# Two graph layers on one core: the first graph's index lists beside the last graph of layer 0, fewer small VectorE operations, and another plan for layer 1

## The chip, the cores and the metric

One core of a Trainium2 chip runs the whole program. The metric is the device time of one execution in microseconds (us), as a median of several runs. Beside it stands one profiled execution, from which every duration of a single instruction comes. The engines are TensorE (PE; its weight load is listed apart as PEld), VectorE (DVE), ScalarE (ACT), GpSimd (POOL) and SyncE (SP, which here only starts transfers). Each engine works through its own instructions in a fixed order and stands still where one of them waits.

## The reference

Two layers are applied in turn to 16 graphs of 1024 nodes with 256 features, each as `x = layernorm(x + layer(x, adj))`. The adjacency is a 0/1 matrix for each graph, about 0.4% ones, denser among the low node numbers.

```python
def layer0(h, adj):                       # h: 16 x 1024 x 256
    Wh = h @ W.T
    att = bn(Wh @ a1 [:, :, None] + Wh @ a2 [:, None, :])
    att = bn(where(att >= 0, att, 0.2 * att))
    att = softmax(att, axis=2) * adj
    return elu(bn(att @ Wh))

def layer1(inputs, adj):                  # 4 heads
    coefs_adj = softmax(adj, axis=-1)
    def head(Wh, w1h, b1h, w2h, b2h, ah, bh):
        fts = inputs @ Wh
        logits = (fts @ w1h + b1h)[:, :, None] + (fts @ w2h + b2h)[:, None, :]
        coefs = ah * softmax(leaky_relu(logits, 0.2) - 1e9 * (1 - adj)) + (1 - ah) * coefs_adj
        return elu(coefs @ fts + bh + inputs)
    return mean over the heads
```

`bn` of the last line of layer 0 takes its mean and variance over all graphs and nodes, so layer 1 of the first graph can only be worked on when the last graph of layer 0 is through.

## The kernel before

**Sizes.** `P` = 128 nodes make a block, `K` = 8 blocks a graph, `C` = 2 halves of the 256 features, `H` = 4 heads, `KH` = 4 blocks half a graph. The adjacency stands in DRAM in bf16 (`adj16`).

**Layer 0** (up to line 662) works in dense form. For each graph 16 steps `n` run (two halves of the nodes, eight blocks each): `aggregate` (line 585, PE, products into `pa`) for this graph, `weights` (538 to 556, ACT and DVE) for the next. A dense transposed mask is loaded two graphs ahead. Tile, the scheduler, orders the instructions here by the program's order and their dependences. After the last `store` (593) lines 648 to 662 make the scale `s3` and shift `t3` of the batch norm.

**Layer 1** is sparse. For every block of 128 target nodes the source nodes that have any edge into it are listed, and padded to whole chunks of 128: `CAPS` = (6, 4, 3, 3, 3, 3, 2, 2) chunks for the eight blocks, 26 in a graph. The lists are made on the chip, for each graph in two halves: `load_rows` (SP) brings rows of `adj16`, `counts` (PE, `pc`) and `used` (DVE) tell which source has an edge into which block, `places` (PE, `pp`) and `placed` (DVE) give each its place, eight `mark` (DVE, line 1153) spread the places as one-hot tiles, `pick` (PE, `pl`) turns these into node numbers, and `indices` (DVE) writes them to `ix` and `im`. With these, POOL's indirect DMAs fetch for each chunk 128 rows of the table `xe_dram` (`fetch_rows`, line 1194, tile `xc`) and 128 mask rows (`fetch_mask`, line 1202, tile `mc`); both have 20 buffers. The masks are rows of `mt_dram`, an f32 copy of the transposed adjacency that POOL's `store_mask` writes from the tile `mt`, of which there is one buffer, filled by a transposing load of SP (`load_mask`).

The table holds, for each node, `x` after layer 0 (lines 1231 to 1346 prepare it: `exps`, `elu`, `turn` with PE's `pz` at line 1250, `residual` with DVE lines 1260 to 1265, `means`, `squares`, `spans` with POOL's power at line 1285, `norm`, `factors`, `raised`, `scale`, `table`, `total`), a one, and exponentials of the attention terms. `rows` brings the targets' factors (`A`, SP), `larger` (ACT, line 1221) and `weights` (DVE, line 1225, tile `w`, 12 buffers) make the edge weights of a chunk for four heads. `neighbours` (PE, line 1347, `pm`) sums each target's neighbours, with the number of them in column 257; `summed` (DVE, 1354 and 1355) and `shares` (DVE, 1359 to 1372) make from it the share of `softmax(adj)`.

**Units.** Each block takes two units of two heads each, 16 (`NU`) for a graph and 256 in all. A unit passes through `gather` (PE, line 1414, `pu`, two PSUM buffers), `share` (ACT, 1424), `sums`, `invert`, `mix` (DVE, 1431 to 1441), `turn` (PE, 1450, `pt`, one buffer), `turned` (ACT, 1456), `linear` (PE, 1462, `pv`, one buffer), `add` (DVE, 1469), `exps` (ACT, 1473), `sum` (DVE, 1480 to 1488), `squares` (ACT), `span` (DVE), `power` (POOL, 1516 and 1517), `close` (ACT, 1523) and `store` (SP, 1529). `addends` (POOL, line 1401, tile `v`) makes x plus bias ahead of `add`.

**The order of layer 1 is written out by hand** (`manual_schedule`): every engine runs its instructions in program order. One turn of the loop near the end is one unit number `n`; it takes the steps of units `n` to `n - 9` in a fixed order, and at three places (`stand(0)`, `stand(1)`, `stand(2)`) the side steps that prepare later graphs, from the lists `early`, `first` and `after`. The side steps of a graph have unit numbers from -30 (30 units before its first) to 15. `turned(n, f, then)` puts PE's step `f` into `first[n]` and its reader on DVE or ACT, `then`, into `early[n + 1]`. All PSUM results of side steps (`pc`, `pp`, `pl`, `pz`, `pm`, `pA`, `pX`) share two buffers (`ps_s`), so such a step waits for the reader of the last but one before it. The weights of a chunk stand in `early`:

```python
after[-7 + 2 * it + j] += [each(g.fetch_mask, c), each(g.fetch_rows, c)]
after[-3 + 2 * it + j] += [each(g.larger, c)]
early[-2 + 2 * it + j] += [each(g.weights, c)]
```

(`it` is the block, `j` the half of its chunks.) Graphs are taken in reverse by `stand`: a later graph's steps stand ahead of an earlier one's.

Of the kernel before, what the change touches and what calls it, by code (L numbers as in the profile page):

```python
# [19 lines left out]
P = 128  # L20
# [7 lines left out]
def kernel(  # L28
# [182 lines left out]


    with ExitStack() as l0:
# [316 lines left out]
        with tc.tile_pool(name="wk", bufs=1) as wk, tc.tile_pool(  # L530
            name="ps_a", bufs=4, space=PSUM
        ) as ps_a, tc.tile_pool(name="ps_s", bufs=2, space=PSUM) as ps_s:
# [85 lines left out]
            if B > 1:  # L618
                queries(1)
            ready1 = {}  # L620
            for b in range(B):
                for n in range(NH * K):
# [6 lines left out]
                    if n == 1:  # L629
                        if b + 2 < B:  # L630
                            mts[b + 2] = mask(mpool, b + 2, "mt0")
                        elif b + 1 == B:
                            ready1[0] = mask(m1pool, 0, "mt1")
                    if n == 1 and b > 0:
                        store(b - 1, NH - 1)
# [402 lines left out]
    with ExitStack() as l1:  # L1038
# [20 lines left out]
        class Graph:  # L1059


            def __init__(self, b):
                self.b = b
                self.S, self.mr, self.xc, self.mc, self.A, self.w = ({} for _ in range(6))
                self.pz, self.pm = {}, {}

# [8 lines left out]

            def load_rows(self, hf):

                self.rw = pk.tile([P, KH, N], BF16, tag="rw", name=f"rw_{self.b}_{hf}", bufs=2)
                nc.sync.dma_start(
                    self.rw, adj16[self.b].rearrange("(q p) j -> p q j", p=P)[:, hf * KH : (hf + 1) * KH]  # L1080
                )
# [12 lines left out]


            def counts(self, hf):

                self.pc = ps_s.tile([P, K, KH], F32, tag="s", name=f"pc_{self.b}_{hf}")
                for k in range(K):
                    for q in range(KH):  # L1100
                        nc.tensor.matmul(
                            self.pc[:, k, q : q + 1], self.rw[:, q, k * P : (k + 1) * P],
                            ones16[:, 0:1], start=True, stop=True,
                        )

            def used(self, hf):

                if hf == 0:
                    self.act = pk.tile([P, K, K], BF16, tag="act", name=f"act_{self.b}", bufs=2)
                nc.vector.tensor_scalar(  # L1110
                    self.act[:, :, hf * KH : (hf + 1) * KH], self.pc, 1.0, None, ALU.min
                )

            def places(self):

                self.pp = pp = ps_s.tile([P, K + 1, K], F32, tag="s", name=f"pp_{self.b}")
                for k in range(K + 1):
                    for kk in range(min(k, K)):
# [563 lines left out]
```

## Time and profile before

| what | value |
|---|---|
| three runs, us | 2762.07, 2766.53, 2776.94 |
| median, us | 2766.53 |
| the profiled execution's own time, us | 2762.28 |
| its span (first to last instruction), us | 2760.0 |
| granted TensorE clock, mean | 0.936 |
| PE, busy us and share of the span | 2452.3, 89% |
| PEld | 1944.1, 70% |
| DVE | 2363.1, 86% |
| ACT | 1832.2, 66% |
| POOL | 1371.1, 50% |
| HBM traffic, GB/s over the span | 172 |

The costliest groups of instructions, with their line, engine, number, busy time and the mean of one:

| line, engine, what | count | busy us | mean ns |
|---|---|---|---|
| 1414 PE, `gather` into `pu` | 3328 | 798.8 | 393 |
| 1225 DVE, `weights` | 1664 | 538.0 | 392 |
| 1221 ACT, `larger` | 1664 | 510.8 | 387 |
| 1462 PE, `linear` into `pv` | 2048 | 489.3 | 382 |
| 585 PE, layer 0's `aggregate` | 1024 | 450.9 | 598 |
| 1202 POOL, `fetch_mask` | 416 | 441.9 | 1062 |
| 1194 POOL, `fetch_rows` | 416 | 418.3 | 1006 |
| 1401 POOL, `addends` | 256 | 305.0 | 1191 |

How to read the profile: a line of a timeline gives the start and the length in us, the engine, the line of the code, the operation, the tile written and those read, the shape, and `xN` where N like instructions in a row are put together; in brackets stands how long the engine was idle before it, and for whom. `L1414` is line 1414. In the list of waits, "PE pz L1250 <- DVE deg L1355: 73.7, 13, 7.0" reads: PE's work on `pz` at line 1250 waited for DVE's `deg` of line 1355, 73.7 us in all, 13 times, at most 7.0. Busy shares are means over stages that have different limits, so each stage is read for itself. The clock in such rows (PEclk) is what was granted to TensorE, as a share of full speed.

### The profile page before, as it was taken

How to read it: one execution, taken by the hardware profiler on the slowest of the kernel's cores; microseconds unless marked ns; L12 is line 12 of the kernel's file. 1: busy time of each engine (PE TensorE's matmuls, PEld its weight loads, DVE VectorE, ACT ScalarE, POOL GpSimd, SP SyncE). 2: the span in 40 equal slices, each digit the busy share in tenths (PEclk: the TensorE clock that was granted, in tenths of full speed). 3: DMA queues.
4: the chain of work that ended last, by engine and by line, in shares of the span. 5: the costliest groups of instructions: out<-in, count | busy, mean ns of one | idle time of the engine just before them, and what ended most of it. 6: DMA issues, size and time to landing. Idle time of an engine off the chain costs nothing. (4 is left out here: it accounts for less than half of the span.)

```text
span 2760.0 us, 44589 instructions
## 1 busy us (share of the span) xinstructions
PE 2452.3 (89%) x14119; PEld 1944.1 (70%) x14119; DVE 2363.1 (86%) x6522; ACT 1832.2 (66%) x4196; POOL 1371.1 (50%) x1442
## 2 busy tenths in 40 slices
PE   7964699999975999889998999999889998999997
PEld 6753354444443888778787887878778887877886
DVE  4347999999943899999999999899999999999997
ACT  1216677777734667677676876767677676776775
POOL 1001000000005768686775867668686775867682
PEclk9985799999976999999999999999999999999999
DMA  9979599756559656658576685756657565674331
GB/s 268 275 173 287 125 233 238 175 159 175 138 184 223 205 115 205 169 146 230 112 209 120 192 198 128 220 112 204 162 150 216 131 205 121 192 193 116 87 85 28
DMA packets 514451, 476.51 MB, mean 173 GB/s; under 512 B 284920, under 2 KB 434464, under 8 KB 508064
## 3 DMA queue, kind: packets, MB, share of 16 engines
q1 hardware_dynamic: 446272, 286.63, 40.2%
q0 software_dynamic: 66720, 184.44, 26.0%
q8 instruction: 115, 1.88, 0.3%
q10 hardware_dynamic: 1216, 2.51, 0.2%
q14 instruction: 128, 1.05, 0.1%
HBM read 304.72 MB, written 168.77 MB: 172 GB/s over the span
## 5 line engine op out<-in xcount | busy, mean ns | idle before, releaser
L1414 PE MATMUL pu<-xc,w 128*128 128x257 f32 x3328 | 798.8, 393 | 0.0
L1414 PEld LDWEIGHTS pu<-xc,w 128*128 128x128 f32 x3328 | 638.5, 198 | 85.4
L1225 DVE SCALAR_TENSOR_TENSOR w<-w,xc,mc 128x128 f32<-128x128 f32 x1664 | 538.0, 392 | 0.3 <-DMA mc<-mt_dram,im 0.3
L1462 PE MATMUL pv<-W1s,sT 128*128 128x256 f32 x2048 | 489.3, 382 | 34.1 <-DVE v L1469 31.6
L1221 ACT ACTIVATE w<-A,xc 128x128 f32<-128x128 f32 x1664 | 510.8, 387 | 12.9 <-DMA xc<-xe_dram,ix 12.9
L1194 POOL DMA_INDIRECT xc<-xe_dram,ix x416 | 418.3, 1006 | 149.0 <-issue 79.5
L1202 POOL DMA_INDIRECT mc<-mt_dram,im x416 | 441.9, 1062 | 99.3 <-issue 92.3
L585 PE MATMUL pa<-em,wh 128*128 128x512 f32 x1024 | 450.9, 598 | 17.7 <-issue 13.4
L1462 PEld LDWEIGHTS pv<-W1s,sT 128*128 128x128 f32 x2048 | 387.3, 191 | 101.0 <-DVE v L1469 46.0
L585 PEld LDWEIGHTS pa<-em,wh 128*128 128x128 f32 x1024 | 193.6, 192 | 250.2 <-issue 236.7
L1456 ACT COPY sT<-pt 128x512 f32<-128x512 f32 x256 | 148.1, 578 | 295.2 <-PE pt L1450 294.1
L1401 POOL TENSOR_TENSOR v<-x,bias 128x512 f32<-128x512 f32 x256 | 305.0, 1191 | 72.6 <-DVE z L1431 67.9
L1424 ACT ACTIVATE s<-S,q 128x256 f32<-128x256 f32 x512 | 230.1, 497 | 131.6 <-DVE q L1372 131.6
L1469 DVE TENSOR_TENSOR v<-pv,v 128x512 f32<-128x512 f32 x256 | 175.1, 684 | 77.4 <-PE pv L1462 74.5
L1441 DVE SCALAR_TENSOR_TENSOR s<-pu,z,s 128x256 f32<-128x256 f32 x512 | 224.3, 480 | 9.1 <-ACT w L1221 0.4
L1347 PE MATMUL pm<-xc,mc 128*128 128x257 f32 x832 | 209.3, 389 | 17.5 <-DMA xc<-xe_dram,ix 17.5
L1473 ACT ACTIVATE m<-v,neg 128x512 f32<-128x512 f32 x256 | 185.0, 723 | 44.0 <-DVE omv L1495 22.4
L541 ACT ACTIVATE e<-eb,c,s 128x1024 f32<-128x1024 f32 x128 | 155.0, 1236 | 79.0 <-DVE sm L555 42.7
L1347 PEld LDWEIGHTS pm<-xc,mc 128*128 128x128 f32 x832 | 155.6, 192 | 42.8 <-issue 11.5
L545 ACT ACTIVATE e<-e,v,u 128x1024 f32<-128x1024 f32 x128 | 152.3, 1229 | 22.7 <-DVE e L544 16.6
L1250 PE MATMUL pz<-IW,h 128*128 128x136 f32 x512 | 88.1, 317 | 87.5 <-DVE deg L1355 78.4
L1450 PE MATMUL pt<-ident,s 128*128 128x128 f32 x1024 | 162.0, 283 | 0.0
(260 smaller groups left out, 3593.8 us busy)
## 6 DMA issues: line engine op xcount, KB each, us to landing
mt_dram<-mt POOLq DMA_DIRECT2D x16, 4096.0 KB
x<-in_x_dram SPq DMA_DIRECT2D x32, 1024.0 KB
adj<-in_adj_dram POOLq DMA_DIRECT2D x16, 2048.0 KB
rw<-adj SPq DMA_DIRECT2D x32, 1024.0 KB
A<-a_dram SPq DMA_DIRECT2D x128, 256.0 KB
xe_dram<-x SPq DMA_DIRECT2D x16, 1060.0 KB
wh_dram<-wx SPq DMA_DIRECT2D x16, 1024.0 KB
wh<-wh_dram SPq DMA_DIRECT2D x16, 1024.0 KB
```

Of the source, the lines that this page charges most:

```text
L585: nc.tensor.matmul(acc[b, hf, oc], wh[b][:, k, oc * P : (oc + 1) * P], ems[b, k][:, hf * HALF : (hf + 1) * HALF], start=(k == 0), stop=(k ...
L1194: nc.gpsimd.indirect_dma_start(out=self.xc[c], out_offset=None, in_=xe_dram[self.b % 2], in_offset=bass.IndirectOffsetOnAxis(ap=self.ix[:, ...
L1202: nc.gpsimd.indirect_dma_start(out=self.mc[c], out_offset=None, in_=mt_dram[self.b % 3].rearrange("n (q i) -> (n q) i", i=P), in_offset=ba ...
L1221: nc.scalar.mul(w[:, h, :], self.A[it][:, h, :], self.xc[c][:, F1 + h : F1 + h + 1])
L1225: nc.vector.scalar_tensor_tensor(self.w[c][:, h, :], self.w[c][:, h, :], self.xc[c][:, F1 + H + h : F1 + H + h + 1], self.mc[c], ALU.max, ...
L1347: nc.tensor.matmul(pm, self.mc[c], self.xc[c][:, 0:F1], start=(c == cs[0]), stop=(c == cs[-1]))
L1401: nc.gpsimd.tensor_tensor(self.v2, self.g.x[:, self.it, 0:F].unsqueeze(1).to_broadcast([P, HP, F]), bias1[:, h : h + HP, :], ALU.add,)
L1414: nc.tensor.matmul(self.pu[:, hh, 0:F1], g.w[c][:, h, :], g.xc[c][:, 0:F1], start=(c == cs[0]), stop=(c == cs[-1]),)
L1424: nc.scalar.mul(self.s[:, hh], g.S[it], g.q[:, it, h0 + hh : h0 + hh + 1])
L1441: nc.vector.scalar_tensor_tensor(s[:, hh], self.pu[:, hh, 0:F], self.z[:, hh : hh + 1], s[:, hh], ALU.mult, ALU.add,)
L1462: nc.tensor.matmul(self.pv[:, hh, :], self.sT[:, hh, fc, :], W1s[:, fc, self.hp * HP + hh, :], start=(fc == 0), stop=(fc == C - 1),)
L1473: nc.scalar.activation(self.m, self.v2, AF.Exp, bias=neg1, scale=1.0)
```

## The change

1. **The lists of graph 0 in layer 0.** The steps of the lists move, unchanged, into a class `Lists` that takes its pools and the number `n` of blocks in a part. Graphs 1 to 15 use it as before (two parts of four). Graph 0's run in layer 0, in four parts of two, at steps 1 to 10 of the last graph; its row tiles take the buffers `e` of layer 0's `weights`, its PSUM tiles come from a new pool `ps_l`. The mask of graph 0 is loaded one graph earlier, and its store to `mt_dram` stands in layer 0; the mask of graph 1 is loaded at step 4 of the last graph.

2. **Mask fetches of graph 0.** The first 14 stand at unit -30, ahead of layer 1's other steps.

3. **Small operations.** The copy of `fs` out of `pz` goes from DVE to ACT (`beside`). `summed` takes all 257 columns at once: the degree stays in `S`, now made in pairs with four buffers, and `X` has the constant `N` as column 257. So the copy to `deg` and the first operation of `shares` are gone.

4. **The plan.** Unit numbers come from a table `AT`. The weights stand in a new list `late`, taken by `stand(3)`, which follows `stand(0)` and `stand(1)`; their unit numbers are the same. Others move by up to three units: `count` 0 from -25 to -23, `pick` 0 from -13 to -11, `elu` 3 and its `exps` from -23 to -22, `turn` 6 from -15 to -16, `nb` (neighbours) 3 and 4 one later, 6 one earlier, `rows` 0 and 3 to 6 one to three earlier and `rows` 1 one later, the fetches of blocks 2 to 5 one or two units away from their old ones, some `larger` by one, and `load_mask`, `load_h`, the second `load_rows`, `mark` 1 and `table` by one.

5. **The order within a unit** is another:

| before | after |
|---|---|
| turn, turned, gather, sums, add, invert, mean, span, mix, exps, stand(0), share, linear, stand(1), sum, squares, stand(2), addends, power, close, store | sums, add, invert, exps, turn, turned, gather, linear, store, mean, span, mix, stand(0), addends, stand(1), stand(3), share, sum, squares, stand(2), close, power |

The diff, cut to its core:

```diff
+    def store_mask(b, mt):
+        nc.gpsimd.dma_start(mt_dram[b % 3][0:N, :].rearrange("(k p) i -> p k i", p=P), mt)
+    class Lists:
+        def __init__(self, b, n, pool, psum, keep, rows):
+            self.b, self.n, self.pool, self.psum, self.keep, self.rows = b, n, pool, psum, keep, rows
+            self.rw, self.oh = {}, {}
+        def load_rows(self, hf):
+            self.rw[hf] = self.rows([P, self.n, N], BF16, f"rw_{self.b}_{hf}")
...
+        def pick(self, hf):
+            qs = range(hf * self.n, (hf + 1) * self.n)
...
@@ layer 0
+            lists0 = Lists(
+                0, 2, lk, ps_l, m1pool, lambda shape, dt, nm: wk.tile(shape, dt, tag="e", name=nm, bufs=4)
+            )
+            beside = {n: [] for n in range(NH * K)}
+            for part in range(K // 2):
+                beside[1] += [lambda part=part: lists0.load_rows(part)]
+                beside[1] += [lambda part=part: lists0.counts(part), lambda part=part: lists0.used(part)]
+            beside[2] += [lists0.places, lists0.placed, lambda: store_mask(0, ready1[0])]
+            for part in range(K // 2):
+                for q in (2 * part, 2 * part + 1):
+                    beside[3 + 2 * part] += [lambda q=q: lists0.mark(q)]
+                beside[4 + 2 * part] += [
+                    lambda part=part: lists0.pick(part), lambda part=part: lists0.indices(part)
+                ]
...
-                        elif b + 1 == B:
+                        elif b + 2 == B:
                             ready1[0] = mask(m1pool, 0, "mt1")
+                    if b == B - 1 and n == 4 and B > 1:
+                        ready1[1] = mask(m1pool, 1, "mt1")
+                    for step in beside[n] if b == B - 1 else ():
+                        step()
@@ residual
-                nc.vector.tensor_copy(self.fs[:, k], self.pz[k][:, :, P:TW])
+            def beside(self, k):
+                nc.scalar.copy(self.fs[:, k], self.pz[k][:, :, P:TW])
@@ totalled
-                self.X = pk.tile([P, F], F32, tag="X", name=f"X_{b}", bufs=2)
-                nc.scalar.copy(self.X, self.px)
-                self.deg = pk.tile([P, K], F32, tag="deg", name=f"deg_{b}", bufs=2)
+                self.X = pk.tile([P, F1], F32, tag="X", name=f"X_{b}", bufs=2)
+                nc.vector.memset(self.X[:, F:F1], float(N))
+                nc.scalar.copy(self.X[:, 0:F], self.px)
@@ summed
-                self.S[it] = pk.tile([P, F], F32, tag="S", name=f"S_{b}_{it}", bufs=6)
-                nc.vector.scalar_tensor_tensor(self.S[it], pm[:, 0:F], E1, self.X, ALU.mult, ALU.add)
-                nc.vector.tensor_copy(self.deg[:, it : it + 1], pm[:, F:F1])
+                if it % 2 == 0:
+                    self.S[it // 2] = pk.tile([P, 2, F1], F32, tag="S", name=f"S_{self.b}_{it}", bufs=4)
+                nc.vector.scalar_tensor_tensor(
+                    self.S[it // 2][:, it % 2], self.pm[it], E1, self.X, ALU.mult, ALU.add
+                )
@@ shares
-                nc.vector.tensor_scalar(r[:, 0], self.deg[:, part], E1, float(N), ALU.mult, ALU.add)
-                nc.vector.reciprocal(r[:, 0], r[:, 0])
-                nc.vector.tensor_scalar(r[:, 1], self.deg[:, part], 0.0, None, ALU.is_equal)
+                d = self.S[pair][:, :, F]
+                nc.vector.reciprocal(r[:, 0], d)
+                nc.vector.tensor_scalar(r[:, 1], d, float(N), None, ALU.is_equal)
@@ side
                 for j, part in enumerate(halves(it)):
                     for c in part:
-                        after[-7 + 2 * it + j] += [each(g.fetch_mask, c), each(g.fetch_rows, c)]
-                        after[-3 + 2 * it + j] += [each(g.larger, c)]
-                        early[-2 + 2 * it + j] += [each(g.weights, c)]
+                        after[AT["fetch", it, j] if g.b or c >= 14 else -EARLY] += [each(g.fetch_mask, c)]
+                        after[AT["fetch", it, j]] += [each(g.fetch_rows, c)]
+                        after[AT["larger", it, j]] += [each(g.larger, c)]
+                        late[AT["weigh", it, j]] += [each(g.weights, c)]
```

## The prediction

> **What bounds the kernel now.** I read the page's 40 slices first: layer 0 fills the first twelve (to 797 us), then a thin slice, then 27 dense ones, layer 1. All numbers are from the one profiled execution (span 2760.0, its own time 2762.28). Next came the table by stretches, over the part of layer 1 in which every graph does the same. Line 1285 runs once per graph; two of its rows, in the timeline of POOL, mark the stretch:
>
> ```profile
> 1035.78 1.68 POOL L1285 TENSOR_TENSOR rs<-rs,mhalf 128x8 f32<-128x8 f32 x1 [16.09 <-DVE r L1361]
> ...
> 2574.71 1.68 POOL L1285 TENSOR_TENSOR rs<-rs,mhalf 128x8 f32<-128x8 f32 x1 [16.43 <-DVE r L1361]
> ```
>
> These are graphs 2 and 15, so 13 periods of 118.4 us. The stretch between them:
>
> ```profile
> core 0: us, PE busy (x) PEld busy (x) DVE busy (x) ACT busy (x) POOL busy (x), PEclk, DMA share, GB/s
> 1036.00:2575.00 1539.00, 1426.62 (x8855) 1249.57 (x8854) 1429.07 (x4502) 1120.34 (x2978) 1089.68 (x1119) 0.96 0.65 168
> ```
>
> Divided by 13, PE is busy 109.7 and DVE 109.9 of 118.4; ACT 86.2, POOL 83.8. Two engines share the bound, and each idles 8.5 us per graph. The list of waits of the same stretch says for whom (total, times, longest):
>
> ```profile
> PE pz L1250 <- DVE deg L1355: 73.7, 13, 7.0
> DVE v L1469 <- PE pv L1462: 65.1, 69, 1.4
> ...
> PE pv L1462 <- DVE v L1469: 24.1, 22, 1.7
> ```
>
> Per graph PE waits 5.7 us once, and DVE waits 5.0 us in five pieces. The timelines of PE and DVE at the end of graph 2's units show the single wait:
>
> ```profile
> 1228.21 0.63 PE L1250 MATMUL pz<-IW,h 128*128 128x136 f32 x4
> 1235.84 1.25 PE L1250 MATMUL pz<-IW,h 128*128 128x136 f32 x4 [7.00 <-DVE deg L1355]
> 1236.88 1.06 PE L1450 MATMUL pt<-ident,s 128*128 128x128 f32 x4
> 1237.73 6.33 PE L1414 MATMUL pu<-xc,w 128*128 128x257 f32 x24
> ```
>
> ```profile
> 1229.02 0.16 DVE L1269 TENSOR_SCALAR mv<-mv 128x4 f32<-128x4 f32 x1
> 1229.09 6.21 DVE L1225 SCALAR_TENSOR_TENSOR w<-w,xc,mc 128x128 f32<-128x128 f32 x12
> 1235.21 0.41 DVE L1354 SCALAR_TENSOR_TENSOR S<-pm,X 128x256 f32<-128x256 f32 x1
> 1235.55 0.14 DVE L1355 COPY deg<-pm 128x1 f32<-128x1 f32 x1
> ```
>
> The second `turn` of unit 15 needs the PSUM buffer of the neighbour sum `pm`, which DVE empties (1354, 1355) only after twelve weights (1225). PE stands 7.0 us, then runs slower for a while: `pz` 1.25 against 0.63, `pt` 1.06 against 0.60, the first `pu` 6.33 against 5.37 for the next unit's 24. That is 2.0 more.
>
> **The change, part by part.** *Weights last.* `weigh` keeps its units but now stands behind every other side step of the unit, so `summed` follows line 1269: it ends at 1229.09 + 0.34 = 1229.4 instead of 1235.6. PE's 7.0 becomes 0.7, and the slow restart's 2.0 goes. What is late next: the first gather needs the weights of chunks 3 to 5, which end at 1229.4 + 6.1 = 1235.5, so PE ends that gather near 1236 to 1238, not at 1243.9; then `linear` waits for DVE's `add`, at 1238.6. PE leads by 5.3 us from there. DVE is at 1237.9 as before, but its later waits for `linear` (0.96, 1.54 and 1.06 within 1254 to 1268 alone) lose their cause. I let all 5.0 per graph go. Bounds: none of it, or DVE's whole idle down to PE's floor.
>
> *Fewer DVE passes.* By start-to-start spacing: eight `fs` copies x 0.09 = 0.7, eight `deg` copies x 0.07 = 0.55, four first ops of `shares` x 0.20 = 0.8; one memset of 0.07 is new, and 257 columns for 256 is one element. 2.0 per graph. The copies go to ACT, where the trace has none of that shape; `ar` (32x128, 0.24) and `X` (128x256, 0.36) bound it: 1.9 to 2.9 us, nearer 1.9, hidden in ACT's idle 32; 2.9 if that were gone.
>
> *Period.* DVE: 109.9 - 2.0 = 107.9 busy, plus 8.5 - 5.0 = 3.5 idle: 111.4, a gain of 7.0. PE: 109.7 - 2.0 = 107.7 busy, so it has 3.7 of room. Bounds: 2.0 (passes alone) to 118.4 - 107.9 = 10.5. The wait occurs at 14 boundaries (the last two graphs have no graph to turn): 14 x 7.0 = 98, bounds 28 to 147. Graphs 14 and 15 keep the passes: 2 x 2.0 = 4, bounds 0 to 8.
>
> *Other moved steps* (one answer): `nb` 3, 4 a unit later and 6 earlier, `turn` 6, `pick` 0, `count` 0, fetches, `larger`, `rows` by one to three units, `addends` ahead of the fetches, `exps` ahead of `turned`, the out store ahead. Their cover is PE's 3.7 us and the idle of ACT (32) and POOL (33). Without it, unit 1's three marks (0.6 each) stand before the buffer of `turn` 7: 1.8 x 14 = 25. On SP, rows of `A` now come in twos behind the same out stores; `load_rows` 0 of the next graph waits for `pick` 0 two units later, and it is needed four units on. I take 0.
>
> *Lists of graph 0.* PE gets, per graph of lists, 30.3/16 for counts, about 1.5 for places (817.5 to 819.0) and 66.0/16 for picks: 7.5 us, in front of aggregates that PE runs without a gap to 796.2; plus waits for the mark chain, 0 to 5: layer 0 ends 8 to 12 later, I take 9. SP gets four `rw` loads, graph 1's transpose (15.7, behind the 4 MB `mt_dram` store that frees its tile) and the load of `x`, ahead of the last `h_dram` store; that store is 12 us away, and each us beyond would count. Between the start of line 1234 (801.9) and line 1315 (831.9) DVE loses 8 us of lists and the waits for `rw` and `x`: elu 4 x 1.62 + 0.7, turns 8 x 1.08, squares 2.8, the power 2.2, factors 1.2, sum 21.5 for 30.0. So the table is written when it was. The gain lies behind it:
>
> ```profile
> 850.29 0.97 POOL L1194 DMA_INDIRECT xc<-xe_dram,ix  x1 [17.29 <-DMA xe_dram<-x]
> ...
> 885.34 2.38 PE L1347 MATMUL pm<-xc,mc 128*128 128x257 f32 x4 [5.47 <-DMA xc<-xe_dram,ix]
> 887.51 2.13 PE L1250 MATMUL pz<-IW,h 128*128 128x136 f32 x8
> ```
>
> Fetches leave every 1.25 us, masks and rows in turn; chunk 9 was twentieth, then waited for its landing under a 22.45 us transpose. Fourteen masks are now fetched before (17.5 us of POOL, 811 to 829, just before the power op is due near 830; later than that, it, the `mt_dram` store of graph 1 and every row fetch move with it). Ten rows take 11.3: chunk 9 leaves at 861.6 for 874. With the landing, the first gather (889.4) comes 12 to 19 earlier, I take 16; bounds 4 to 25.
>
> Sum: 16 + 98 + 4 = 118: 2762.3 - 118 = 2644. The profiled run lies 4.2 below the median of the three (2766.53), so 2648.
>
> **A rule against the change.** One line's instructions show a collision:
>
> ```profile
> 1282.06 1.75 DVE L1486 SCALAR_TENSOR_TENSOR o<-x,v 128x256 f32<-128x256 f32 x1
> ...
> 1282.25 1.28 POOL L1401 TENSOR_TENSOR v<-x,bias 128x512 f32<-128x512 f32 x1
> ```
>
> The same op takes 0.42 at 1266.0. Means over usual values (1225: 392 for 346 ns x 104; 1486: 659 for 425 x 8; 1244, 1483, 1488, 1153, 1372 alike) give DVE 10.6 us of it per graph, of at most 16 x 1.19 = 19.1 for line 1401. The reorder moves that line; I keep 10.6, since POOL runs up to 16 us ahead of DVE and meets it at no fixed place. The Trainium skill (SBUF — State Buffer, "SBUF: two separate sides") says that VectorE with two SBUF inputs and GpSimd share one port pair as an exclusive lock: whoever starts first keeps it for the whole instruction, the other stands. By it the new place could cost anything from no collision (PE's floor, 2599) to all (8.5 more per graph, 2767).
>
> **Rivals.** *Forecast, 0.57:* 2648, own range 2615 to 2690 (period 109 to 114). *The wait only moves, 0.20:* gather and `pv` take the whole lead, DVE keeps its idle; for it: 24.1 us already wait on `add`; against: PE leads where DVE's waits lie. Gain 14 x 2.0 + 20 = 48: 2718. *Floor, 0.08:* 14 x 10.5 + 20 = 167: 2599; for it, both engines reach it; against, loads differ by unit. *More collisions, 0.10:* weights stand in one block where `addends` now falls, all sixteen collide and half of the 8.4 us of lines 1516 and 1517: 8.5 + 4.2 = 12.7 on 111.4, 5.7 above 118.4: 14 x 5.7 - 20 = 60 slower, 2827. It decides from 8.4 more per graph. *Nothing comes, 0.05:* SP's queue delays layer 1's start and the lead is lost too: about 2760.
>
> **From these to the numbers.** The likeliest is 2648; 2598 to 2722 takes in the floor and the moved wait and leaves the last two out. Three cases are faster by over 0.5% (about what a measurement here tells from none): 0.85, with 0.05 and 0.10.
>
> **What would show it.** Right: PE's wait on `pm`'s reader under 1.5 us, the power op every 111 us, DVE's wait for `linear` under 1.5 per graph, layer 0's last `pa` near 805, the first `pu` near 873. Wrong: a new wait of several us once per graph on PE, mean times of lines 1225 and 1486 above 0.42 and 0.75, or a table written after 842.

## The result, and the profile after

The changed kernel took 2859.15 us, median of four runs (2846.63 to 2864.26), against 2764.3 us for the kernel before, a ratio of 1.033 (95% interval 1.028 to 1.039): slower, where 2648 was forecast. The same program, measured three more times, took 2730.9 and 2727.7 us on two chips (both 0.988, within 0.985 to 0.991) and 2885.4 us on a third (1.039, 1.034 to 1.044), while the kernel before stayed between 2761 and 2777 us everywhere. The chip of the first measurement isn't recorded; it may be the third. So there are two things to explain: why only 30 to 35 of the forecast 118 us come even in the two better measurements, and what takes another 130 to 160 us in the two others.

The first measurement's profile has a span of 2844.9 us. The power operation, now line 1319, runs at 1032.8 for graph 2 and at 2661.2 for graph 15: 13 periods of 125.3 us, 118.4 before. The table by stretches over just that part (the columns as before: the stretch, its length, the busy time of each engine with its number of instructions, TensorE's clock, the share of the DMA engines):

```profile
core 0: us, PE busy (x) PEld busy (x) DVE busy (x) ACT busy (x) POOL busy (x), PEclk, DMA share, GB/s
1032.80:2661.20 1628.40, 1452.39 (x8851) 1254.74 (x8850) 1376.12 (x4255) 1123.78 (x3080) 1086.43 (x1119) 0.94 0.62 160
```

Per graph VectorE is busy 105.9 us (109.9 before) and TensorE 111.7 (109.7): the passes are gone, and yet they now idle 13.5 us (TensorE) and 19.4 us (VectorE), some 8.5 each before. The same 13 periods in the second measurement, the first of the two better ones, take 118.1 us each:

```profile
1013.40:2548.40 1535.00, 1408.22 (x8854) 1234.96 (x8854) 1346.64 (x4255) 1127.64 (x3082) 1124.97 (x1118) 0.95 0.66 170
```

There TensorE is busy 108.3 us per graph and VectorE 103.6. The list of waits of the first measurement's stretch (who waited for whom, us in total, times, longest; the one named after the arrow is the record that ended last before the wait did, and need not be the one that was waited for):

```profile
PE pm L1381 <- DMA xc<-xe_dram,ix: 104.0, 13, 10.2
...
POOL mt_dram L215 <- DMA mt<-adj: 77.7, 13, 7.7
DVE S L1391 <- PE pm L1381: 67.2, 14, 8.0
...
POOL xc L1226 <- DMA mt_dram<-mt: 60.2, 13, 5.8
...
DVE v L1509 <- PE pv L1502: 27.3, 24, 1.6
DVE act L248 <- PE pu L1452: 23.3, 8, 3.3
...
DVE most L268 <- PE pu L1452: 17.7, 4, 5.2
...
DVE most L268 <- PE pt L1490: 14.9, 4, 5.1
```

Of the two waits that the forecast looked at, TensorE's for the neighbour sum's reader at the turn (`pz`) has shrunk from 73.7 to 12.2 us, and in the second measurement it is gone. VectorE's for `linear` (`v` from `pv`) is 27.3 us here for 65.1 before, but in the second measurement it stands nearly as it was:

```profile
DVE v L1509 <- PE pv L1502: 56.6, 40, 1.6
```

New is a wait of TensorE, 8.0 us once per graph, for fetched rows at a neighbour sum, with VectorE behind it (`S`), and two of POOL around the mask store. The second measurement has these too (113 us of TensorE over its 13 periods). Only the first of the two has VectorE's waits for the counts (`act`) and the places (`most`).

The place of the old wait, in TensorE's timeline at the end of a graph's units, shows that the weights' move did what it should:

```profile
1629.77 0.73 PE L1282 MATMUL pz<-IW,h 128*128 128x136 f32 x4 [0.18 <-ACT fs L1299]
1630.33 1.46 PE L1381 MATMUL pm<-xc,mc 128*128 128x257 f32 x6
1631.63 0.60 PE L1490 MATMUL pt<-ident,s 128*128 128x128 f32 x4
1632.07 5.37 PE L1452 MATMUL pu<-xc,w 128*128 128x257 f32 x24
```

Instead of 7.00 us the turn waits 0.18, and `pt` and `pu` run at 0.60 and 5.37 us, without the slow restart. The new wait stands seven units on. Four timelines of the same graph (its first `sums` at 1633.3) show its chain, SP, ACT, POOL and PE:

```profile
1639.63 9.06 SPq L1243 DMA_DIRECT2D A<-a_dram  x2
1648.79 15.20 SPq L1210 DMA_TRANSPOSE mt<-adj  x1
```

```profile
1647.02 1.27 ACT L1253 ACTIVATE w<-A,xc 128x128 f32<-128x128 f32 x4
```

```profile
1668.95 0.97 POOL L215 DMA_DIRECT2D mt_dram<-mt  x1 [6.52 <-DMA mt<-adj]
1670.23 1.06 POOL L1234 DMA_INDIRECT mc<-mt_dram,im  x1 [0.31 <-issue]
1671.60 0.97 POOL L1226 DMA_INDIRECT xc<-xe_dram,ix  x1 [0.30 <-issue]
...
1673.85 0.95 POOL L1234 DMA_INDIRECT mc<-mt_dram,im  x1 [0.16 <-issue]
1675.11 0.95 POOL L1226 DMA_INDIRECT xc<-xe_dram,ix  x1 [0.30 <-issue]
```

```profile
1688.34 2.05 PE L1381 MATMUL pm<-xc,mc 128*128 128x257 f32 x4 [8.21 <-DMA xc<-xe_dram,ix]
```

In the kernel before, the same places of a graph (its first `sums` at 1600.9), SP, POOL and PE:

```profile
1590.35 18.19 SPq L1074 DMA_TRANSPOSE mt<-adj  x1
```

```profile
1632.65 0.97 POOL L1174 DMA_DIRECT2D mt_dram<-mt  x1 [0.25 <-issue]
```

```profile
1661.51 1.03 PE L1347 MATMUL pm<-xc,mc 128*128 128x257 f32 x4
```

In the changed kernel two rows of `A` stand ahead of the transposing load on SP. The second, for block 5, gets its buffer when ScalarE has done the last edge weights of block 2, at 1648.3; 0.5 us later the load starts, 15.5 us after the first `sums`, where in the kernel before it started 8 to 11 us ahead of them. So it is not done when POOL comes to the mask store, which waits 6.5 us, and the two fetches of block 6 stand behind that store. They issue at 1671.6 and 1675.1, 38 and 42 us after the first `sums`, on the mean of the graphs 2 us later than in the kernel before. But the neighbour sum of block 6 now stands a unit earlier: TensorE comes to it 47 us after the first `sums`, waits 8.2 us for the last of the fetches and begins at 55, where it began at 60 in the kernel before.

At the start of layer 1 the row fetches came as forecast (the first at 849.6, the tenth at 861.0), but the first gather did not come at 873: it came at 892.6. VectorE's timeline there, and below it that of the second measurement of the same program:

```profile
867.15 0.19 DVE L248 TENSOR_SCALAR act<-pc 128x32 bf16<-128x32 f32 x1 [12.22 <-remote]
883.30 0.43 DVE L1391 SCALAR_TENSOR_TENSOR S<-pm,X 128x257 f32<-128x257 f32 x1 [15.95 <-remote]
```

```profile
855.33 0.19 DVE L248 TENSOR_SCALAR act<-pc 128x32 bf16<-128x32 f32 x1 [0.94 <-PE pc L239]
862.83 0.43 DVE L1391 SCALAR_TENSOR_TENSOR S<-pm,X 128x257 f32<-128x257 f32 x1 [7.31 <-PE pm L1381]
```

"remote" is a wait that no recorded instruction ends. The counts `pc`, 32 matmuls of one column, are in TensorE's record from 854.9 to 855.8 in the first trace, and VectorE reads their result at 867.15. The neighbour sum behind them ends in the record at 863.1, and VectorE reads it (`S`) at 883.3.

### The profile page after: what moved, and what is told of

Its sections match the earlier page's. It is cut to its first block, busy times and chain, and to the rows that moved or that the text cites. A ratio compares the mean times of both kernels' runs of the same rounds, so it can differ in the third digit from the quotient of the medians.

```text
span 2844.9 us, 44259 instructions
## 1 busy us (share of the span) xinstructions
PE 2475.3 (87%) x14119; PEld 1945.8 (68%) x14119; DVE 2300.3 (81%) x6224; ACT 1837.8 (65%) x4324; POOL 1374.5 (48%) x1442
## 5 line engine op out<-in xcount | busy, mean ns | idle before, releaser
L1452 PE MATMUL pu<-xc,w 128*128 128x257 f32 x3328 | 783.8, 387 | 3.6 <-issue 3.6
L1452 PEld LDWEIGHTS pu<-xc,w 128*128 128x128 f32 x3328 | 627.5, 195 | 86.1 <-issue 5.8
L1257 DVE SCALAR_TENSOR_TENSOR w<-w,xc,mc 128x128 f32<-128x128 f32 x1664 | 577.9, 414 | 2.7 <-ACT w L1253 1.5
L1226 POOL DMA_INDIRECT xc<-xe_dram,ix x416 | 438.1, 1053 | 223.5 <-issue 93.6
L1234 POOL DMA_INDIRECT mc<-mt_dram,im x416 | 435.4, 1047 | 109.5 <-issue 103.0
L1439 POOL TENSOR_TENSOR v<-x,bias 128x512 f32<-128x512 f32 x256 | 318.3, 1244 | 194.1 <-DVE z L1471 192.0
L1381 PE MATMUL pm<-xc,mc 128*128 128x257 f32 x832 | 238.3, 429 | 106.2 <-DMA xc<-xe_dram,ix 105.1
L1381 PEld LDWEIGHTS pm<-xc,mc 128*128 128x128 f32 x832 | 167.3, 212 | 136.3 <-issue 104.3
L215 POOL DMA_DIRECT2D mt_dram<-mt x16 | 15.5, 971 | 341.4 <-DMA mt<-adj 341.4
```

Of the source, the lines that this page charges most:

```text
L1226: nc.gpsimd.indirect_dma_start(out=self.xc[c], out_offset=None, in_=xe_dram[self.b % 2], in_offset=bass.IndirectOffsetOnAxis(ap=self.l.ix[ ...
L1234: nc.gpsimd.indirect_dma_start(out=self.mc[c], out_offset=None, in_=mt_dram[self.b % 3].rearrange("n (q i) -> (n q) i", i=P), in_offset=ba ...
L1257: nc.vector.scalar_tensor_tensor(self.w[c][:, h, :], self.w[c][:, h, :], self.xc[c][:, F1 + H + h : F1 + H + h + 1], self.mc[c], ALU.max, ...
L1381: nc.tensor.matmul(pm, self.mc[c], self.xc[c][:, 0:F1], start=(c == cs[0]), stop=(c == cs[-1]))
L1439: nc.gpsimd.tensor_tensor(self.v2, self.g.x[:, self.it, 0:F].unsqueeze(1).to_broadcast([P, HP, F]), bias1[:, h : h + HP, :], ALU.add,)
L1452: nc.tensor.matmul(self.pu[:, hh, 0:F1], g.w[c][:, h, :], g.xc[c][:, 0:F1], start=(c == cs[0]), stop=(c == cs[-1]),)
```

## The experiments

The theory: SP's queue (theory Q in the texts below) makes the mask's load late, and all else follows. Rivals: the neighbour sum of block 6 is simply one unit too early (N); POOL's `addends` ahead of the fetches make these late (A). Beside these stands the forecast's main step, alone on the kernel before. The kernel before took 2762.7 us beside the first four.

**SP's queue as before.**

```diff
-            'lm': -29,
+            'lm': -30,
...
-                do(n - 9, "store")
                 do(n - 5, "mean")
...
                 do(n - 7, "power")
+                do(n - 9, "store")
```

> The changed kernel with SP's queue as before: the out store again the last step of a unit, the mask of a later graph again loaded at unit -30. Theory Q (SP's queue): in the profile of the changed kernel the transposing load of the mask starts 15.5 us after a graph's first sums instead of 8.3 before, POOL waits 5 to 7 us for it at the mask store, the fetches of block 6 stand behind that store, and PE waits 7.5 us per graph for them at the neighbour sum of block 6. Q expects the load back near -8, no wait of POOL at the mask store, PE's wait for the last fetch of block 6 under 2.5 us, a period of 112 to 118 instead of 125.3, and 2670 to 2770 us. Rival N (the plan number alone: the neighbour sum of block 6 stands one unit too early for its fetches): PE still waits over 5 us there, period above 122, time above 2810. Rival A (POOL's addends ahead of the fetches make the fetches late): as N.

Measured: 2615.3 us, ratio 0.947 (0.945 to 0.948). The load starts at -6.6, POOL doesn't wait at the mask store and comes to it at 28.6, the two fetches leave at 31.6 and 35.6, and TensorE doesn't wait at the neighbour sum, which still stands at unit 7. The period is 109.4 us. Q stands in its direction, but gained 55 us more than its range allowed; N and A fall as the only cause.

**The neighbour sum of block 6 a unit later.**

```diff
-            ('nb', 6): 7
+            ('nb', 6): 8
```

> The changed kernel with one number of the plan back: the neighbour sum of block 6 at unit 8 instead of 7. Theory Q: POOL still waits 5 to 7 us at the mask store and the fetches of block 6 leave as late as now (41 us after the first sums, landing near 63), so PE's wait there falls from 7.5 to about 1, but what else hangs on the late fetches and on late loads stays: period 118 to 122, 2740 to 2810 us. Rival N: the wait goes whole and nothing else was wrong: period 112 to 116, 2660 to 2730. Rival A: PE waits on for later fetches, over 4 us per graph, above 2810.

Measured: 2690.1 us, 0.973 (0.971 to 0.975), period 115.2. POOL still waits, 6 to 10 us, at the mask store; TensorE's wait falls to between 0.4 and 3.4 us. These are N's numbers; Q's were reckoned from the first 2859 us, which the later measurements put some 130 too high. But N's ground, that nothing else was wrong, doesn't hold: the first experiment takes the wait away with the neighbour sum where it was, and the next one has a period 6.4 us shorter than this.

**Both.**

> Both edits in one: SP's queue as before, and the neighbour sum of block 6 at unit 8. Theory Q: within 0.5% of SP's queue alone, 2660 to 2765 us, since the wait is gone with either. Rival N: within 0.5% of the plan number alone. Rival A: above 2790, with PE still waiting for fetched rows.

Measured: 2607.3 us, 0.944 (0.942 to 0.946), period 108.8. With the load early, the number of the neighbour sum is worth 8 us in the whole run: within 0.5% of SP's queue alone, as Q said, though below its range. This is the fastest version of all.

**The weights last, alone, on the kernel before.**

```diff
-                        early[-2 + 2 * it + j] += [each(g.weights, c)]
+                        late[-2 + 2 * it + j] += [each(g.weights, c)]
...
                 stand(1, n)
+                stand(3, n)
```

> The kernel before with one part of the change alone: the twelve or so weights of a unit stand behind all its other side steps, at the same unit numbers. The forecast's own step: PE's 7.0 us wait for the neighbour sum's reader goes to under 1.5, DVE's waits for the linear products shrink, 5.0 us per graph or 70 in all: 2695 us, at least below 2740. Rival M (the wait only moves: PE then waits for the weights at the first gather of a graph, DVE keeps its 8 us of idle): within 0.5% of the kernel before.

Measured: 2693.0 us, 0.974 (0.972 to 0.976): 70 us, as the step said, and 66 in a repetition (2697.8, the last experiments). The waits of TensorE in this kernel, 1036 to 2400 us:

```profile
PE pv L1462 <- DVE v L1469: 36.7, 26, 2.6
PE pu L1414 <- DVE w L1225: 10.8, 12, 1.7
PE pz L1250 <- DVE deg L1355: 10.8, 12, 1.0
```

The 7.0 us at `pz` are now 0.9 (10.8 in 12), and the gather waits 0.9 per graph for its weights: rival M, by which the wait only moves, would have put 5 us there. VectorE's wait for `linear` falls to 0.6 us per graph.

The next four take the two SP edits apart, put them on the kernel before, and run the changed kernel again. The kernel before beside them: 2761.4 us.

**The changed kernel again.**

> The changed kernel once more, as it is. Its profile has 78 us of waits that no recorded instruction ends, all of them for TensorE results that came up to 16 us after the records of the matmuls that make them (28 us at the start of layer 1, then five times 6 to 8 us on ScalarE's copy of the turned shares); neither the kernel before nor the four experiments so far have any. Theory P (a property of this program: TensorE falls behind after long waits for fetched rows): such waits come again, 2820 to 2870 us. Theory C (chance of one chip or run): none or few, and 2770 to 2820 us, since 125.3 a graph with PE's 7.5 us wait at the neighbour sum stays and only the lost 28 us and some 8 us waits go.

Measured: 2730.9 us, 0.988 (0.985 to 0.991), four runs from 2726 to 2734, period 118.1. No "remote" wait is in the trace, the first gather comes at 871.0, and TensorE still waits for fetched rows, 102 us between 1036 and 2400. Theory C in its sign; its 2770 to 2820 us were 40 too high.

**The mask's load alone back at unit -30.**

```diff
-            'lm': -29,
+            'lm': -30,
```

> The changed kernel with the mask of a later graph loaded at unit -30 instead of -29, the out store still ahead. Theory Q: with both edits the load started at -6.6 us from the graph's first sums and POOL's mask store left at 28.6 without waiting; with this one alone the load should start 6 to 8 us earlier than in the changed kernel (15.5), so near 8, and end near 24, before POOL comes to it: no wait at the store, 2615 to 2680 us. If the out store's place is the greater part (theory O), the load stays above 12, POOL waits over 2 us, 2700 us or more.

Measured: 2616.7 us, 0.948 (0.945 to 0.951). The load starts at 6.4 and ends at 17 to 19, POOL comes at 28.6 and doesn't wait. One unit number is worth 114 us. Over its 13 periods, in the table by stretches and SP's timeline:

```profile
985.40:2409.50 1424.10, 1393.57 (x8858) 1212.17 (x8857) 1363.04 (x4255) 1126.21 (x3082) 1122.13 (x1119) 1.00 0.69 184
```

```profile
1537.53 10.82 SPq L1210 DMA_TRANSPOSE mt<-adj  x1
1548.44 1.53 SPq L1243 DMA_DIRECT2D A<-a_dram  x2
```

Here the load stands ahead of the two rows of `A`, not behind them. TensorE is busy 107.2 us of 109.5 and VectorE 104.8.

**The out store alone back at the end of a unit.**

```diff
-                do(n - 9, "store")
                 do(n - 5, "mean")
...
                 do(n - 7, "power")
+                do(n - 9, "store")
```

> The changed kernel with the out store the last step of a unit again, the mask still loaded at unit -29. Theory Q: the load starts near 0 to 2 us from the first sums and ends by 18, POOL doesn't wait at the mask store at 28.6, and the time is within 1% of both edits together, 2605 to 2640 us. If one unit later of the load is the greater part, POOL waits there and the time is above 2700.

Measured: 2751.5 us, 0.996 (0.994 to 0.998), ten runs. The load still starts at 15.5, POOL waits 8 to 10 us and TensorE 8 to 13. The expectation fails: the out store's place is not what made the load late. It moves the load by 13 us where nothing else holds it (-6.6 against 6.4 in the first and fifth experiment), and that costs nothing, as the load is done by 19.

**The two SP edits on the kernel before.**

> The kernel before with the two edits of SP's queue alone: the out store moved ahead, the mask loaded one unit later. Theory Q: the load goes from -8.3 to about 14 us after the first sums and ends near 30; POOL comes to the mask store of this kernel only at 33.6, so hardly a wait there, and the sum of block 6 stands a unit later than in the changed kernel: 2755 to 2800 us. Rival W (late loads cost whatever stands behind them, through the rows of targets and the out store's own waits): above 2800 us.

Measured: 2761.8 us, 0.999 (0.998 to 1.001). The load starts at 6 to 8 there, not at 14, and nobody waits for it. So one unit later alone isn't the cause either: something else of the plan holds the load in the changed kernel. SP's timeline above names it: the row of block 5, moved from unit 5 to unit 2.

The next three test that, and two more parts alone. The kernel before beside them: 2762.3 us.

**The rows of block 5 back at unit 5.**

```diff
-            ('rows', 5): 2
+            ('rows', 5): 5
```

> The changed kernel with one number of the plan back: the target rows of block 5 loaded at unit 5 instead of 2. What the last runs left: with the mask's load at unit -29 (unit 3 of the graph two before), giving the out store its old place helped nothing (load at 15.5 us, 2751 us), while unit -30 helped all (2617). Theory R: the rows of block 5, now at unit 2, wait on SP for a buffer that ScalarE frees only in unit 2 (block 2's edge weights), and the load at unit 3 stands behind them; at unit 2 it stands ahead. R expects the load to start under 11 us, POOL's wait at the mask store under 1 us, 2610 to 2640 us. If the load's own unit number is what counts (theory U), it stays near 15, POOL waits 6 us, 2715 to 2745 us.

Measured: 2645.9 us, 0.958 (0.956 to 0.960). The load starts at 6.3 to 7.1: theory R, though the time lies 6 us above its range. The load lasts until 20 to 26, and in three graphs TensorE still waits for fetched rows (7.1 us in one, behind 3.6 us of POOL at the mask store); those periods are 113 to 117 us, the others 110 to 111. 82 of the 114 us come back against the changed kernel measured beside it (2727.7); the rest goes with a load that ends too late in some graphs, while the neighbour sum of block 6 has no unit to spare.

**Fewer VectorE passes, alone, on the kernel before.**

```diff
-                nc.vector.tensor_copy(self.fs[:, k], self.pz[k][:, :, P:TW])
+            def beside(self, k):
+                nc.scalar.copy(self.fs[:, k], self.pz[k][:, :, P:TW])
...
-                nc.vector.tensor_copy(self.deg[:, it : it + 1], pm[:, F:F1])
...
-                nc.vector.tensor_scalar(r[:, 0], self.deg[:, part], E1, float(N), ALU.mult, ALU.add)
```

> The kernel before with the fewer VectorE passes alone (fs copied by ScalarE, degree kept as column 257 of the neighbour sum). The forecast's step: 2.0 us of VectorE per graph, the bound shared by two engines, so 1.0 to 2.0 us per graph or 16 to 32 us: 2730 to 2745. Rival H (hidden: VectorE's saving becomes idle, since PE's wait for the reader of the neighbour sum and the product buffers set the period): within 0.3% of the kernel before. Rival X (the copy on ScalarE frees the buffer of the turned rows later, so PE waits): slower.

Measured: 2745.3 us, 0.992 (0.989 to 0.995): 17 us, period 117.3 for 118.4; 20 us (2744.5) in a repetition, period 116.4 in its trace. Between the two: VectorE's busy time falls by 1.0 us per graph in the first trace and by 1.9 in the second, and the period by 1.1 and 2.0. TensorE's wait at the turn stays, 5.3 and 5.8 us per graph.

**All lists in layer 1, with the mask's load at unit -30.**

```diff
-                    for step in beside[n] if b == B - 1 else ():
-                        step()
...
-                self.l = lists0 if b == 0 else Lists(
+                self.l = Lists(
...
-                        after[AT["fetch", it, j] if g.b or c >= 14 else -EARLY] += [each(g.fetch_mask, c)]
+                        after[AT["fetch", it, j]] += [each(g.fetch_mask, c)]
```

> The changed kernel with the mask's load at unit -30 (2617 us) and the first graph's lists made in layer 1 as in the kernel before, its mask fetches in turn with the row fetches, its mask loaded with the last graph. The forecast's step: lists in layer 0 bring the first gather 16 us earlier and make layer 0 9 us longer; measured 870.3 for 889.4 and 803 for 796. Expected: first gather near 889, layer 0's last aggregate near 796, and 16 to 20 us slower than with them, 2633 to 2640. Rival H: the first graph's later units fill the gap, under 8 us: 2617 to 2625.

Measured: 2632.6 us, 0.953 (0.951 to 0.954); first gather at 885.4, layer 0's last aggregate at 795.2. Against 2616.7 with the lists in layer 0 that is 16 us, with layer 0 8 us shorter and the first gather 13 us later.

**The changed kernel a third and a fourth time.** The third beside the last three, the fourth beside the version with the load at unit -30.

> The changed kernel a third time. The same program took 2859 us in the first measurement and 2731 in the second, on another chip, with the kernel before at 2764 and 2761. Theory C (the late TensorE results of the first measurement belong to that chip or its state): 2715 to 2745 us here, no waits without a recorded cause. Theory P (they belong to the program and come by chance): 2800 or more in some runs, spread over 2%.

> The changed kernel a fourth time. In the first measurement VectorE waited 58 us (15 times) for the counts and 52 us (12 times) for the places, results of bursts of 32 and 52 small bf16 matmuls, besides 16 us at the start of layer 1; in two measurements since, on two other chips, 0.9 us in all, and 2731 and 2728 us. Theory C (that chip or its state): 2715 to 2745 us and no such waits, unless it is the same chip. Theory P (the program, by chance): 2800 or more here or there.

> The changed kernel with the mask's load at unit -30, again, beside the run above on the same chip: 2617 us before. Theory C: 2605 to 2630 where the changed kernel takes 2715 to 2745; if the changed kernel is late here, this one shows whether the lateness needs PE's waits for fetched rows (then 2617 still) or comes with the small matmuls alone (then 2700 or more).

Measured: 2727.7 us the third time (0.988, 0.985 to 0.990); the fourth time, on another chip, 2885.4 us in two runs (1.039, 1.034 to 1.044), with the kernel before at 2776.6 there. The version with the load at -30 took 2763.9 us on that chip (eight runs from 2737 to 2783; 0.996, 0.992 to 0.999), against 2616.7. All runs of a measurement are late together, so it isn't the chance of a single run, though those of the load at -30 spread by 1.7%. And the version without waits for fetched rows is late on the third chip as well.

What is late there: VectorE's waits of over 0.3 us for the counts and the places in layer 1, added up from the traces (the kernel before makes the first graph's lists there too, and its figures hold them):

| kernel, measurement | us | for the counts | for the places |
|---|---|---|---|
| changed, first | 2859 | 58 (15 times) | 52 (12) |
| changed, second and third | 2731, 2728 | 0.9 (1) | 0 |
| changed, fourth | 2885 | 61 (15) | 106 (14) |
| load at -30 | 2617 | 0.9 (1) | 0 |
| load at -30, beside the fourth | 2764 | 50 (17) | 62 (9) |
| before, first and again | 2762, 2769 | 5.9 (3) | 0.8 (1) |

One of them, in the timelines of TensorE and VectorE of the first measurement (the places are 52 matmuls of eight columns, from 1482.73):

```profile
1484.49 0.20 PE L257 MATMUL pp<-act,ones 128*128 128x8 bf16 x2 [0.49 <-issue]
...
1485.31 0.17 PE L257 MATMUL pp<-act,ones 128*128 128x8 bf16 x1 [0.39 <-issue]
1485.35 1.99 PE L1381 MATMUL pm<-xc,mc 128*128 128x257 f32 x8
```

```profile
1492.66 0.16 DVE L268 TENSOR_TENSOR most<-most,pp 128x8 f32<-128x8 f32 x1 [6.61 <-PE pv L1502]
```

In the second measurement the same burst shows no gap, and VectorE reads the places without a wait. In the first measurement, and in both traces from the third chip, TensorE takes in the last matmuls of most such bursts in small groups, one per 0.7 to 0.8 us, and the results come 3 to 9 us late. Not only these: the turned shares `pt` made behind the burst, in TensorE's record until 1487.9, reach ScalarE late too:

```profile
1494.29 0.59 ACT L1496 COPY sT<-pt 128x512 f32<-128x512 f32 x1 [7.57 <-remote]
```

Some thirty times in the first measurement ScalarE stands idle until 2 to 7 us after the record of such shares, and not once in the second. So what is late is TensorE's work from the burst on, not the small matmuls' results alone. What one late burst costs can be read from the version with the load at -30 on the third chip: the eight periods in which VectorE waits 6.6 to 8.1 us for the places last 118.8 to 119.9 us, the five without such a wait 111.2 to 111.4.

**Which part of the change brings that.** The kernel before, two parts of the change alone on it, and the version with the load at -30 and all lists in layer 1, on one chip.

> The kernel before, for its trace. On one chip the changed kernel took 2885 us (2731 and 2728 on two others) and its variant with the mask's load at unit -30 2764 (2617), while the kernel before took 2777 (2761, 2762); the two changed ones waited 112 to 167 us there for the small matmuls of the lists. If this call meets such a chip: theory S (the small matmuls run late on it only in the changed order of work) expects under 20 us of such waits here and 2770 to 2790 us. Theory L (they run late here too, but VectorE's wait is covered by its idle): over 60 us of lateness, little of it waited for. On a chip like the others: 6 to 7 us of such waits, 2760 us, nothing told.

> The kernel before with the weights last alone (2693 us before). On a chip of the slow kind: if the fuller TensorE is what makes the small matmuls late, over 60 us of waits for them and 2750 or more; if not, 2690 to 2710. On the others 2693.

> The kernel before with the fewer passes alone (2745 us before). On a chip of the slow kind: over 60 us of waits for the small matmuls if the copy on ScalarE or the changed readers bring the lateness, else 2745 to 2765.

> The changed kernel with the mask's load at unit -30 and all lists in layer 1 (2633 us before). On a chip of the slow kind: 2760 to 2790 if order or plan bring the lateness, near 2650 if the lists in layer 0 do. On the others 2633.

Measured: 2769.5 us (1.002, 1.001 to 1.003), 2697.8 (0.976), 2744.5 (0.992) and 2648.2 (0.958), each within 0.6% of what it took before; waits for counts and places about 7 us in all four. The chip was like the others, and the question stays open.

## Why the prediction was wrong, point by point

**The weights last: right where it stood alone.** 70 us were priced for it (5.0 per graph), and alone it gave 70 and 66. TensorE's 7.0 us went to 0.9 there and VectorE's waits for `linear` to 0.6 us per graph. In the changed kernel TensorE's wait went too, but VectorE's for `linear` stayed at 4.4 us per graph in the second measurement, where TensorE stands 8.7 us per graph for fetched rows; with the load at -30, without that wait, it is 1.8.

**Fewer passes: the size off where they stand alone.** 32 us were priced (2.0 per graph), 17 and 20 measured. What came off VectorE's busy time came out of the period (1.0 and 1.1 us, 1.9 and 2.0), but in the first trace only half of the 2.0 came off: some of its other operations ran longer there (the elu's four 1104 ns for 972). Why is not shown.

**The lists in layer 0: right.** Layer 0 ended at 802 to 805 (forecast near 805), the first gather came at 870 to 873 on the chips without late results (forecast near 873), and taking it back costs 16 us (forecast 16). The terms from elu to factors add up to 22.0, not to the 21.5 given; nothing rests on the half us, as the power operation came at 828.5 for 828.9.

**"Other moved steps ... I take 0": the step that failed.** It saw the moves and priced them by cover: "On SP, rows of `A` now come in twos behind the same out stores", "`nb` 3, 4 a unit later and 6 earlier", and the cover named was TensorE's 3.7 us and the idle of ScalarE and POOL. What it did not ask of each moved transfer is what it waits for and what stands behind it on its queue. `rows` 5 at unit 2 waits for a buffer that is freed at the end of block 2's `larger`, itself at unit 2; `load_mask`, which stands one unit behind it now and would stand ahead of it at its old number, inherits that wait and starts 9 us later (22 with the out store in its old place in both); the mask store on POOL inherits it from the load; the fetches of block 6 stand behind the store; and the neighbour sum of block 6 was moved a unit ahead. In the kernel before it began at 60 us with its last fetch issued at 38 to 41, and did not wait; in the changed kernel TensorE comes to it 13 us earlier, the fetch leaves 2 us later, and from the fetch's issue to the sum's start pass 12 to 15 us. None of this is busy time on any engine, so no engine's idle covers it. Undoing the one number of the load gives back 114 us, that of the rows 82, that of the neighbour sum some 40 (2690.1 for 2727.7, the same chip at different times).

**The sum.** Without that one move the forecast's range would have held on the chip of the second measurement: with the load at -30 the kernel takes 2617 us there (forecast 2648, 2598 to 2722), with a period of 109.5 us for the forecast 111.4; on the chip of the fourth it takes 2764. That it comes so near is in part luck. The parts tried alone add up to 70 + 17 + 16 = 103 us of the 145; the other 42 no step had. In the trace of that version VectorE is busy 104.8 us per graph, 3.1 less than the forecast's 107.9, and idles 4.7 for the forecast's 3.5; 3.1 over 14 periods are 43 us. Operations that the change leaves as they are take less there than in the kernel before (the elu's four 681 ns for 972, the 104 edge weights 380 for 389, one operation of the places 198 for 1051). Whether the new order does that, or the parts together, was not taken apart.

**The rivals.** More collisions (2827) came near the first number for the wrong reason: VectorE's surplus from working beside POOL, by such a sum of means over usual values, is 9.6 us per graph in the first experiment, against 10.6 before, so the new place of `addends` costs nothing there. In the changed kernel's first and second traces it is 10.4 and 7.9, and the mean times named as signs of it stay below them (414 and 382 ns for the edge weights, 532 and 710 for `o`). The wait that only moves (2718) came near the other measurements, for the wrong reason as well: the lead went to a transfer, not to the gather. "Nothing comes" named SP's queue, but only for layer 1's start, and there the fetches left on time. Of the signs named for a wrong forecast, "a new wait of several us once per graph on PE" is the one that came.

**The first number.** About 130 us of the 2859 go with TensorE's late results. VectorE's waits for the counts and places (58 + 52 us) and 9 us more than in the second measurement for the neighbour sum at the start of layer 1 come near that, but they are not the whole account: of the 7.2 us by which the period is longer than in the second measurement, VectorE idles 4.9 more and is busy 2.3 more. No step and no rival had this, and the two traces of the kernel before show none of it (it was not traced on the third chip, where it took 2776.6). Shown is where the lateness begins, behind the bursts of small matmuls, that it came in two measurements of four, and that the waits for fetched rows are not needed for it. What brings it on there, and which part of the change makes the program open to it, is not settled. That TensorE's instructions come slowly to it in these bursts, as the gaps marked "issue" could mean, or that it works through them more slowly than its records say, was not tested.

## What to carry to other kernels

A transfer that is moved in a queue is priced by what it waits for and by everything behind it on that queue, up to the consumer that has the least time to spare; idle time of engines covers work, not lateness. When a planner moves a load whose buffer is freed late, look which load now stands behind it. Measure a changed kernel on more than one chip before a few per cent are put down to the change.

## What the hardware showed unasked

TensorE's granted clock is 1.00 over the 13 periods of the version with the load at -30, where TensorE's longest wait is 1.2 us, 0.99 with the weights last alone (2.6), 0.96 in the kernel before (7.0) and 0.94 and 0.95 in the changed kernel's first and second measurements (10.2 and 11.0). With the waits of several us gone, TensorE is busy 107.2 us per graph, against 109.7 in the kernel before and 108.3 in the second measurement; the 111.7 of the first holds the late results as well. The Trainium skill (TensorE: Matmul & The Clock Gate, "Part 1: The HAM clock gate") says that the array falls back to half its clock after an idle window of about 3.4 us and comes back after as long a busy one. These clocks agree with it, and so do the first matmuls behind a 7.0 us wait in the kernel before, 1.25 us for 0.63.

In the first measurement the end of a matmul in the trace lies 11 us ahead of the reading of its result (the counts, 855.8 and 867.15) and once 20 us (the neighbour sum, 863.1 and 883.3). The Trainium skill (Perfetto Trace Analysis, "Tensor Engine Instruction (MATMUL, LD_WEIGHTS)") says that this end is an estimate from the instruction's size, not observed. In these traces the reader's start is the safer mark.
